# Roots of the last norms one at a time, a routing moved ahead of a sum, and a routing in four matmuls, at the end of a one-layer attention and expert kernel

## The chip, the cores and the metric

The kernel runs on one core of one Trainium2 chip. The metric is the device time of one execution in microseconds (us). Three runs of the kernel before took 838.86 us in the median, from 838.44 to 840.26. Engines are named as in the profile: PE is TensorE (matmuls), PEld its loading of weights, DVE is VectorE, ACT is ScalarE, POOL is GpSimd, SP is SyncE, which only issues DMAs here.

## What is computed

Two sequences of 512 tokens with 512 features go through one layer: attention with 32 query heads in 8 groups, a residual and a layer norm, then a feed-forward step with a small mixture of low-rank experts, a residual and a second layer norm. Everything is float32. The change lies in the last two lines of this:

```python
x = _layernorm(x + attention(x))
# feed-forward, four active experts of rank 8
y = einsum('bth,oh->bto', x, W_base) + b_base
z = einsum('bth,erh->bter', x, lora_A[active])
alpha = softmax(log(domain_prior[active] + 1e-12) + (einsum('bth,eh->bte', x, router_W) + router_b)[..., active])
x = _layernorm(x + y + einsum('bteo,bte->bto', einsum('bter,eor->bteo', z, lora_B[active]) * 2.0, alpha))
```

## The kernel before, in words

The tokens lie in eight tiles of 128 rows, four for each sequence. The attention runs as a long sequence of slots, `slot(T)`, each of which issues a little of every stage (projection, scores, exponentials, transposes through DRAM, context, output projection). The order in which instructions are issued is the order of the program text: nothing rearranges it, every engine works through its own instructions in that order and waits by semaphores for the others. Work for the feed-forward step is hung into the last slots with `put`. After the last slot a block written out by hand (from line 1020 on) finishes the last five tiles. The change is in this block and in the helpers it calls.

The tiles of the first sequence are `f0`, the last of which is `fz`. The four tiles of the second sequence finish in the order `fa[0]`, `fa[1]`, `fb`, `fc`; below they are also written fa0, fa1, fb and fc. Each tile is an `Ffn` object and goes through these steps:

- `base(c)`, for four chunks c of the features (line 686, tile `py`): x times the base weights, in two halves of 256 output columns, with the low-rank input (16 columns for each half) and the router's logits (4 columns) carried in the same matmuls. So the widths are 272 and 276.
- `logits` (L703 and L705, tiles `lg` and `nmx`): adds the prior and takes the maximum over the four experts.
- `alphas` (L712 to L717): the exponential on ACT with its sum, then on DVE the reciprocal, the scale, and two multiplications that give `zs`, the weighted low-rank activations.
- `low_rank` (L726, L727): PE transposes `zs` into a bank that all tiles share, DVE copies it to `zT`.
- `finish` (L731): two matmuls of `zT` with the second low-rank factors, added to `py`.
- `add` (L737): the sum with the residual into `y`, then `norm2.stats` (L634, L635).
- `norm2.root(lo, hi)` (L638, L639): for the columns lo to hi of a norm that several tiles share, the square root on ACT and then the reciprocal on DVE.
- `store` (L642, L764): POOL applies the norm to `y`, and SP issues the DMA of the tile to the output.

The tile `fc` is treated otherwise: `route` (L696, tile `zl`) computes only its low-rank input and logits, in eight matmuls of 16 or 20 columns, so that its `alphas` can be had early. Its product comes later in halves (`half`, `half_end`, L745 to L752, tile `ph`), with the residual added by a matmul with the identity, and its statistics are read from the bank (L755).

Square root and exponential need different function tables on ACT. A load of a table is put in front of an activation that needs another table than the one before it; it appears in the profile under the line of that activation. Copies on ACT need none.

A matmul of float32 operands appears in the profile as two records (two passes), a transpose as one.

Of the kernel before, what the change touches and what calls it, by code (L numbers as in the profile page):

```python
# [9 lines left out]
F32 = mybir.dt.float32  # L10
# [5 lines left out]
P = 128  # L16
# [13 lines left out]
def postln_layer_kernel(  # L30
# [33 lines left out]
    nc = tc.nc  # L64
    B, S, HID = x.shape
    NT = B * S // P
    TPB = S // P
    KC = HID // P
# [3 lines left out]
    EA = active.shape[0]  # L72
    EAR = EA * RK
# [44 lines left out]
    OH, ARH = O // 2, EAR // 2  # L118
    WX_COLS = OH + ARH + EA
    arT = const.tile([P, KC, EAR + EA], F32, name="arT")  # L120
# [503 lines left out]
    class Norm:  # L624
# [10 lines left out]
            nc.vector.bn_aggr(self.mv[:, i, :], st)  # L635

        def root(self, lo, hi):
            nc.scalar.activation(self.rstd[:, lo:hi], self.mv[:, lo:hi, 1], AF.Sqrt, bias=eps_sb)  # L638
            nc.vector.reciprocal(self.rstd[:, lo:hi], self.rstd[:, lo:hi])  # L639

        def apply(self, i, dst, src=None, engine=nc.vector):
# [10 lines left out]
    class Ffn:  # L652
# [28 lines left out]
        def base(self, c):  # L681
            if c == 0:
                self.new_banks()
            for n in range(2):
                w = OH + (ARH, WX_COLS - OH)[n]
                nc.tensor.matmul(  # L686
                    self.py[n][:, :w], lhsT=self.xT[:, c, :], rhs=wbT[:, c, n, :w], start=(c == 0), stop=(c == KC - 1),
                    skip_group_check=True)

        def route(self, pool, tag):  # L690

            zl = pool.tile([P, 2, WX_COLS - OH], F32, tag=tag, name="zl")
            for n in range(2):
                w = (ARH, WX_COLS - OH)[n]
                for c in range(KC):
                    nc.tensor.matmul(  # L696
                        zl[:, n, :w], lhsT=self.xT[:, c, :], rhs=wbT[:, c, n, OH : OH + w],
                        start=(c == 0), stop=(c == KC - 1))
            self.z = [zl[:, n, :] for n in range(2)]

        def logits(self):
            self.lg = self.own([P, EA], "lg")
# [272 lines left out]
    wbT = ffn_pool.tile([P, KC, 2, WX_COLS], F32, name="wbT")  # L975
# [9 lines left out]
    def tiles(ts_, banks, name):  # L985
        n = len(ts_)
        norms = Norm(ffn_pool, n, f"a{name}"), Norm(ffn_pool, n, f"f{name}")
        return [Ffn(t, bank, *norms, i) for i, (t, bank) in enumerate(zip(ts_, banks))]

    f0 = tiles(range(TPB), ((QX, QY), (QX, QY), (SC, SC), (QX, QY)), "0")  # L990
    fa = tiles([TPB + i for i in order[:2]], ((SC, SC), (WX, WY)), "1a")
# [28 lines left out]
    fz = f0[3]  # L1020
# [37 lines left out]
    fz.finish()  # L1058
    fc.transpose(*CTX)
    fz.add()  # L1060
    base(fa[1])
    fa[0].low_rank()
    fc.route(*CTX)
# [3 lines left out]
    fa[1].alphas()  # L1067
    fa[0].finish()
    fa[0].add()
    for c in range(KC):  # L1070
        fb.base(c)
        if c == 2:
            fa[1].low_rank()
    fc.low_rank()
    fa[1].finish()
    fa[1].add()
    fz.norm2.root(3, TPB)
    fa[0].norm2.root(0, 2)
    for f in (fz, *fa):
        f.store()  # L1080
    fb.logits()
    fb.alphas()
    for c in range(KC):
        fc.half(0, c)
    fc.half_end(0)
    fc.half_stats(0)
    fb.low_rank()
    for c in range(KC):
        fc.half(1, c)
# [59 lines left out]
```

## Time and profile before

| | |
|---|---|
| three runs, median (lowest to highest) | 838.86 us (838.44 to 840.26) |
| the profiled execution's own time | 839.75 us |
| its span, first to last instruction | 838.0 us |
| PE busy | 825.9 us, 99% |
| DVE busy | 595.6 us, 71% |
| ACT busy | 354.3 us, 42% |
| POOL busy | 290.1 us, 35% |
| mean granted clock of PE | 0.996 |
| table loads on ACT from 790 us to the end | 7, of 1283 ns each |

The span counts from the first to the last instruction; the execution's own time is 1.75 us longer. Times inside the profile are given in us from the start of the span. The profile has several views: the rows of the whole span; the chain of work that ended last, followed back from the last instruction through whatever released each step; a timeline of each engine, in which square brackets give the idle time of the engine before a row and what ended it; and a table by stretches, with busy time of each engine and the granted clock of PE (1.00 is full speed). Ends of matmuls are modelled, so lengths of PE's rows overlap somewhat.

### The profile page before, as it was taken

The numbers are of one execution on the slowest core, as the hardware profiler recorded it, in microseconds if no ns is written. First come the engines' busy times: TensorE is split into PE (matmuls) and PEld (weight loads), VectorE is DVE, ScalarE is ACT, GpSimd is POOL, SyncE is SP. The second block draws the span as 40 slices with busy tenths as digits, with TensorE's granted clock in tenths as the row PEclk, the third lists the DMA queues.
The fourth block names the chain that finished last, engine by engine and source line by source line (L and its number), as shares of the span: only waits on it lengthen the run. The fifth ranks groups of instructions, "written<-read, shape, count | busy, mean of one in ns | idle before, by whom it ended". The sixth has DMA issues, their size and how long they took to land.

```text
span 838.0 us, 10735 instructions
## 1 busy us (share of the span) xinstructions
PE 825.9 (99%) x3201; PEld 583.9 (70%) x3201; DVE 595.6 (71%) x1964; ACT 354.3 (42%) x1002; POOL 290.1 (35%) x318
## 2 busy tenths in 40 slices
PE   8999999999999999999999999999999999999996
PEld 5566677777777777777777777777777776655574
DVE  5468977787767967686767866687767878964535
ACT  1225454534434444444434343444435344663133
POOL 6463344233322334232332334334333523300022
PEclk9999999999999999999999999999999999999998
DMA  9126536364553556263543557274544536574211
GB/s 289 39 63 190 157 83 194 103 177 123 151 148 102 166 152 194 62 175 115 151 138 105 172 148 193 61 204 143 152 125 126 177 90 199 163 247 118 63 39 63
DMA packets 84971, 116.47 MB, mean 139 GB/s; under 512 B 6581, under 2 KB 64797, under 8 KB 82866
## 3 DMA queue, kind: packets, MB, share of 16 engines
q1 hardware_dynamic: 84258, 115.50, 48.1%
q0 software_dynamic: 448, 0.14, 0.2%
q8 instruction: 25, 0.41, 0.2%
q14 instruction: 32, 0.26, 0.1%
q10 hardware_dynamic: 208, 0.15, 0.1%
HBM read 71.73 MB, written 44.04 MB: 138 GB/s over the span
## 4 chain that ended last, share of the span: by engine, by line
PE 90%; DVE 4%; DMA 2%; ACT 1%; issue 1%; POOL 1%; SPq 0%; DVEq 0%; POOLq 0%
PE pc L544 16%; PE sc L488 13%; PE qx L429 11%; PE wx L429 11%; PE pp L355 9%; PE qy L429 8%; PE wy L429 8%; PE pv L342 6%; PE py L686 3%; PE po L615 3%; DMA pT<-db 1%; PE tp L274 1%; PE py L731 1%; DMA db<-zt 1%; DMA x_sb<-_attn_hidden_states_dram 1%
## 5 line engine op out<-in xcount | busy, mean ns | idle before, releaser
L503 ACT ACTIVATE p<-sc,nmax 128x288 f32<-128x288 f32 (+15 forms) x256 | 124.4, 486 | 253.0 <-DVE nmax L496 207.5
L496 DVE CUSTOM_DVE_ANT_0 sc<-sc,maskw 128x288 f32<-128x288 f32 (+15 forms) x256 | 114.1, 446 | 154.5 <-PE sc L488 151.7
L544 PE MATMUL pc<-pT,v 128*128 128x512 f32 x320 | 165.5, 599 | 0.6 <-DMA pT<-db 0.6
L488 PE MATMUL sc<-kT,qT 128*128 128x160 f32 (+15 forms) x512 | 162.0, 398 | 1.2 <-ACT p L503 1.1
L376 POOL TENSOR_TENSOR qT<-q,t 128x512 f32<-128x512 f32 x56 | 71.0, 1268 | 188.8 <-DVE q L375 188.8
L511 ACT ACTIVATE p<-p,den 128x288 f32<-128x288 f32 (+15 forms) x256 | 133.4, 522 | 0.1
L488 PEld LDWEIGHTS sc<-kT,qT 128*128 128x128 f32 x512 | 96.7, 190 | 30.3 <-issue 14.3
L416 POOL TENSOR_TENSOR cs<-ctxT 128x256 f32<-128x256 f32 x28 | 26.5, 948 | 196.2 <-PE wy L429 109.5
L550 ACT COPY ctxT<-pc 128x512 f32<-128x512 f32 x64 | 37.5, 586 | 124.9 <-PE pc L544 124.9
L519 DVE STREAM_TRANSPOSE zt<-p 128x128 f32<-128x128 f32 (+2 forms) x192 | 81.6, 425 | 0.0
L544 PEld LDWEIGHTS pc<-pT,v 128*128 128x128 f32 x320 | 57.0, 190 | 19.7 <-issue 5.4
L355 PE MATMUL pp<-xT,wk 128*128 128x512 f32 x128 | 65.0, 593 | 0.5 <-ACT xT L275 0.5
L342 PE MATMUL pv<-wv,xT 128*128 128x256 f32 x256 | 63.6, 379 | 0.0
L429 PE MATMUL wx<-wo,ctxT 128*128 128x256 f32 x224 | 57.7, 380 | 0.4 <-DVE den L507 0.4
L429 PE MATMUL qx<-xs,wq 128*128 128x256 f32 x224 | 58.0, 381 | 0.0
L342 PEld LDWEIGHTS pv<-wv,xT 128*128 128x128 f32 x256 | 48.5, 190 | 13.4 <-issue 6.9
L521 DVE STREAM_TRANSPOSE zt<-p 128x32 f32<-128x32 f32 (+3 forms) x256 | 57.4, 224 | 0.0
L429 PEld LDWEIGHTS qx<-xs,wq 128*128 128x128 f32 x224 | 41.4, 190 | 22.3 <-issue 16.0
L429 PEld LDWEIGHTS wx<-wo,ctxT 128*128 128x128 f32 x224 | 42.4, 190 | 13.5 <-issue 7.7
L503 ACT ACTIVATION_READ_ACCUMULATOR p<-sc,nmax 128x1 f32 x256 | 49.9, 195 | 0.0
L601 DVE TENSOR_TENSOR x_sb<-wx,x_sb 128x256 f32<-128x256 f32 x112 | 46.9, 419 | 0.0
L368 DVE SCALAR_TENSOR_TENSOR t<-q,bqkT,rope_sb 64x512 f32<-64x512 f32 x56 | 43.0, 768 | 1.3
(190 smaller groups left out, 1362.9 us busy)
## 6 DMA issues: line engine op xcount, KB each, us to landing
db<-zt SPq DMA_DIRECT2D x64, 256.0 KB, 4.1
pT<-db SPq DMA_DIRECT2D x16, 1024.0 KB, 4.8
db<-zt SPq DMA_DIRECT2D x64, 192.0 KB, 3.2
pT<-db SPq DMA_DIRECT2D x16, 768.0 KB, 4.5
wq<-in_L_attn_Wq_dram SPq DMA_DIRECT2D x20, 512.0 KB, 4.7
wo<-in_L_attn_Wo_dram SPq DMA_DIRECT2D x10, 1024.0 KB, 7.6
db<-zt SPq DMA_DIRECT2D x64, 128.0 KB, 2.4
pT<-db SPq DMA_DIRECT2D x16, 512.0 KB, 4.1
```

The source lines that it names most:

```text
L342: nc.tensor.matmul(psq["v", gg, t], lhsT=xT[:, c, ts(t, P)], rhs=wvs[gg][0][:, c, :], start=(c == 0), stop=(c == KC - 1))
L355: nc.tensor.matmul(psq[key], lhsT=wt[:, c, cols], rhs=xT[:, c, ts(b, S)], start=(c == 0), stop=(c == KC - 1))
L376: nc.gpsimd.tensor_tensor(dst, t1[:].rearrange("p (n s) -> p n s", s=BLK), t2[:].rearrange("p (n s) -> p n s", s=BLK), ALU.add)
L429: nc.tensor.matmul(ps, lhsT=wt[:, c, :], rhs=xt[:, c, :], start=start and c == 0, stop=c == CH - 1, skip_group_check=True)
L488: nc.tensor.matmul(sc[s][:, :w], lhsT=qT[u][:, i * QB + n].rearrange("p r s -> p (r s)"), rhs=kT[u][:].rearrange("p n s -> p (n s)")[:, :w ...
L496: nc.vector.tensor_tensor_reduce(sc[s][:, :w], sc[s][:, :w], maskw[:, S - w :], -SCALE, -MASKED, ALU.add, ALU.min, nmax[s])
L503: nc.scalar.activation(ptile[s][:, :w], sc[s][:, :w], AF.Exp, bias=nmax[s], scale=-1.0, accum_out=rden[s])
L511: nc.scalar.activation(ptile[s][:, :w], ptile[s][:, :w], AF.Copy, scale=rden[s])
L519: nc.vector.transpose(z[:, :, last - i : last, n, :].rearrange("p q j s -> p j q s"), ptile[s][:, : i * P])
L521: nc.vector.transpose(z[:, : n + 1, last, n, :], ptile[s][:, i * P : w])
L544: nc.tensor.matmul(psc[p], lhsT=v_sb[g // VG, b * TPB + j][:, ts(g % VG, D)], rhs=pT[p][:, :, ts(j, P)], start=(j == 0), stop=(j == i))
L601: nc.vector.tensor_tensor(into, pw[k, bank], into, ALU.add)
```

## The change

Three edits, all in what happens after the last slot:

1. The second norms of fz, fa0 and fa1 were rooted together, after all three sums: one root for fz, one for the pair fa0 and fa1. Now each has its own, put in right after (or one step after) its own sum, and each tile is stored at once. To let the ACT half and the DVE half stand in different places, `root` is split into `sqrt` and `invert`.
2. The `logits` and `alphas` of fb stood behind the sum of fa1 and the three stores. They now stand ahead of fa1's `finish` and `add`.
3. `route` of fc uses four matmuls of 36 columns, with the combined low-rank and router weights `arT`, in place of eight of 16 or 20 columns from `wbT`.

On ACT the order at the end becomes: root of fz, exponentials of fc and fa1, root of fa0, exponential of fb, root of fa1, root of fb and the rest; before, it was exponentials of fc and fa1, roots of fz and of the pair, exponential of fb, root of fb and the rest.

```diff
         def root(self, lo, hi):
+            self.sqrt(lo, hi)
+            self.invert(lo, hi)
+
+        def sqrt(self, lo, hi):
             nc.scalar.activation(self.rstd[:, lo:hi], self.mv[:, lo:hi, 1], AF.Sqrt, bias=eps_sb)
+
+        def invert(self, lo, hi):
             nc.vector.reciprocal(self.rstd[:, lo:hi], self.rstd[:, lo:hi])
...
         def route(self, pool, tag):
 
-            zl = pool.tile([P, 2, WX_COLS - OH], F32, tag=tag, name="zl")
-            for n in range(2):
-                w = (ARH, WX_COLS - OH)[n]
-                for c in range(KC):
-                    nc.tensor.matmul(
-                        zl[:, n, :w], lhsT=self.xT[:, c, :], rhs=wbT[:, c, n, OH : OH + w],
-                        start=(c == 0), stop=(c == KC - 1))
-            self.z = [zl[:, n, :] for n in range(2)]
+            zl = pool.tile([P, EAR + EA], F32, tag=tag, name="zl")
+            for c in range(KC):
+                nc.tensor.matmul(zl, lhsT=self.xT[:, c, :], rhs=arT[:, c, :], start=(c == 0), stop=(c == KC - 1))
+            self.z = [zl[:, :ARH], zl[:, ARH:]]
...
     fz.add()
+    fz.norm2.root(3, TPB)
+    fz.store()
     base(fa[1])
     fa[0].low_rank()
     fc.route(*CTX)
...
     fa[0].add()
+    fa[0].norm2.sqrt(0, 1)
     for c in range(KC):
         fb.base(c)
         if c == 2:
             fa[1].low_rank()
     fc.low_rank()
+    fa[0].norm2.invert(0, 1)
+    fa[0].store()
+    fb.logits()
+    fb.alphas()
     fa[1].finish()
     fa[1].add()
-    fz.norm2.root(3, TPB)
-    fa[0].norm2.root(0, 2)
-    for f in (fz, *fa):
-        f.store()
-    fb.logits()
-    fb.alphas()
+    fa[1].norm2.sqrt(1, 2)
     for c in range(KC):
         fc.half(0, c)
     fc.half_end(0)
     fc.half_stats(0)
+    fa[1].norm2.invert(1, 2)
+    fa[1].store()
     fb.low_rank()
```

## The prediction

> **What bounds the kernel now.** I read the whole-span rows first, then the chain that ended last over its final 30 us, then the timeline of the same stretch engine by engine, and last the table by stretches with the granted clock. PE is busy for 99% of the span, so until the last tiles nothing but a matmul decides. The change touches only the text from the last norms on (about 811 us to the end at 838.0), so its worth is read there. Tile names as in the kernel: fz is the last tile of the first sequence; fa0, fa1, fb, fc (objects fa[0], fa[1], fb, fc) are the four of the second, in the order in which they finish.
>
> The chain, in order of time: start, length, what.
>
> ```profile
> 814.77 1.70 PE zl L696 x16
> 816.47 1.06 PE py L731 x4
> 817.53 4.65 PE py L686 x12
> 822.18 0.11 PE tz L726
> 822.29 0.93 PE py L686 x4
> ...
> 824.88 0.71 DVE st L634
> ...
> 825.82 0.29 ACT rstd_f1a L638
> ...
> 826.14 1.28 ACT L712
> ...
> 827.43 0.40 ACT al L712 x2
> ```
>
> Up to 823.97 the chain is PE. Then it leaves PE: fa1's sum and statistics on DVE, a root on ACT, a table load of 1.28 us, the exponential of fb, and back to PE only at 828.62. In that time PE runs out of work, and its row says for what:
>
> ```profile
> 828.62 0.29 PE L726 MATMUL tz<-ident,zs 128*32 128x128 f32 x1 [1.26 <-DVE zs L717]
> 830.44 0.85 DVE L737 TENSOR_TENSOR y<-py,x_sb 128x256 f32<-128x256 f32 x2 [1.21 <-PE py L731]
> ```
>
> fb's base product was complete at 823.2, so its routing stood ready for 3 us and only its place in the queues held it. From fb's sum at 830.44 to the end nothing changes, so I measure the change by when that sum starts.
>
> The second finding is in the table by stretches (PE, PEld, DVE, ACT, POOL busy, then the clock); I cut it at the clock's own edges.
>
> ```profile
> 814.09:817.50 3.41, 3.41 (x25) 2.81 (x23) 0.76 (x4) 0.39 (x2) 0.00 (x0) 1.00 0.00 0
> 817.50:820.91 3.41, 3.41 (x9) 2.58 (x9) 2.73 (x13) 1.97 (x4) 0.00 (x0) 0.50 0.00 0
> 820.91:824.33 3.42, 3.42 (x17) 2.28 (x15) 1.07 (x4) 0.00 (x0) 0.00 (x0) 1.00 0.00 0
> 827.74:831.15 3.41, 2.53 (x11) 1.73 (x12) 1.97 (x8) 1.36 (x2) 3.41 (x3) 1.00 0.26 100
> ```
>
> For one stretch of 3.41 us the clock was halved. fb's first twelve passes took 4.65 us there; elsewhere sixteen take 3.70 us, 0.231 each, so twelve should take 2.78: 1.87 us lost on the chain.
>
> **The change, part by part.**
>
> *Routing of fc in four matmuls.* A float32 matmul is two passes, so 16 passes become 8, each of 36 columns. A pass of 16 or 20 columns takes 1.70/16 = 0.106 us, the same for both, and a transpose of 128 columns 1.33/12 = 0.111; so 36 columns cost 0.106 to 0.111 and the weights, not the columns, are paid for. Eight fewer: 0.85 us off PE, directly on the chain. The routing weights are now read from the array they were copied from; no new wait.
>
> *fz's root and store between exponentials.* Added on ACT: a load of the root's table and, after the root (0.29), one of the exponential's, 1.28 each. The sum of fz is done at 812.50, ACT is idle from 811.59 to 816.89 (wait of 5.30 for fc's logits). Load to 812.88, root to 813.17, load to 814.46; fc's exponential comes at 816.89 - 0.85 = 816.04. Cost nothing, with 1.6 us of cover; without that cover 2.9 us. DVE's reciprocal (0.13) falls at 813.2, ahead of a copy at 814.81: DVE waits there 2.31 us anyway. POOL's 2.08 us for fz and its store on SP's queue move from 826 to 813; both queues are empty there.
>
> *fa0's root alone.* ACT loads the root's table already at 818.74, 0.85 earlier now; the root must wait for fa0's statistics, which end at 821.08 - 0.85 = 820.23. So root 820.26 to 820.55, then the load for fb's exponential to 821.85. That load is only moved; the exponential of fb is queued behind it. One more root (0.29) and one more reciprocal (0.16) exist because fa's pair is split. After fb's exponential comes another load and the root of fa1; the load that stood there before (827.84) is the same one. So the net is two loads more, both around fz's root.
>
> *fb's routing ahead of fa1's sum.* DVE now does, after fa0's statistics (820.23): copy of fa1's zT to 820.53; copy of fc's zT; reciprocal; logits of fb; their maximum; then waits for ACT. Behind this wait on DVE stand fa1's sum and statistics, fc's first half statistics and fb's zT. Here is the sum with a full clock, every length from the rows of before:
> PE: routing of fc ends 815.6, finish of fa0 to 816.68, twelve passes of fb to 819.46, transpose, four passes to 820.50, transpose of fc at 820.55 (behind the zT copy), finish of fa1 to 821.76, fc's half 1.71 + 0.43 + 0.43 to 824.33, fb's transpose without a wait, four passes to 825.3.
> DVE: fc's zT 820.75, maximum of fb done 821.58. ACT: exponential at 821.87, bound by the load by 0.29 us. DVE, with the distances of 827.43 onward: 822.29 reciprocal, 822.49, 822.76 zs, fa1's sum 822.93, statistics 823.82 and 824.55, fc's half 824.77 (its bank is full at about 824.6), fa1's reciprocal 825.2, fb's zT 825.4 to 825.68.
> PE: finish of fb at 825.72, some 0.4 us after it could have begun: the old wait of 1.26 goes and this one comes. fb's sum follows 0.67 us later (829.77 to 830.44 before), at 826.39 instead of 830.44: 4.05 us.
> The parts: routing 0.85; half clock 1.87; the wait of 1.26 and the issue gaps around it, with the new wait of 0.4 taken off, some 1.3.
>
> *The stores.* fz, fa0 and fa1 leave POOL earlier, at about 815.4, 823.3 and 827.5; the last outputs then share the DMA engines with less. They landed in 1.7 and 1.9 us, the others in 2.0 (median), so I take 0; a gain of at most 0.2 us, no loss.
>
> **The half clock, weighed.** In the stretch before the slow one PE was "busy" throughout, but with the routing: at 0.231 us for 272 columns, 16 passes of 16 or 20 columns are 0.24 us of column work in 1.70. With finish (0.87 of columns in 1.06) and what is left of fa1's base product (0.57) and a transpose, columns filled about 1.8 of 3.41 us, half. The stretch at 827.74, with 0.88 us wholly empty, kept a clock of 1.00 and had about 0.6. [...]
>
> **The table loads, weighed.** [...] The rows show 1.28 and no drain: load at 826.14, next activation at 827.43. [...]
>
> **Numbers.** The profiled execution took 839.75 us, 838.0 of span and 1.75 around it. 839.75 - 4.05 = 835.7. That run stood 0.89 over the median of 838.86. The same reckoning without the half clock puts before at 839.75 - 1.8 = 837.95, 0.5 below the fastest run shown (838.44), so runs without the dip may be a little slower than the sum; I add half of that: **836.0**. If the median run of before had no dip, the gain is only 828.65 - 826.39 = 2.25, which gives 836.6 from 838.86: the same case within its scatter.
>
> **Rivals.**
> - *The dip stays or moves* (20%): 839.75 - 2.65 = 837.1, to 837.4 if it falls on fa1's finish as well. [...] Against: fewer thin passes are left.
> [...]
> - *Slower* (5%): one mechanism, at the four switches between fc's routing and fb's exponential. With x us for a switch fb's exponential starts at 814.06 + 4x once nothing covers them (x over 2.07). At x = 2.97 the gain is gone, from x = 3.16 the time is over 840.5, at 3.3 it is 841.1. Everything behind DVE's wait moves with it. Against: all seven loads of the tail took 1283 ns.
> - *As worked out* (64%): 835.2 to 836.9.
>
> A measurement of this kernel can tell about 0.2% from no change, 1.68 us: faster is under 837.18, slower over 840.54. Faster: all of the first case and over half of the dip's, 0.77; same 0.18; slower 0.05. The range goes from 834.9 (the scatter of before's runs below the sum) to 837.9, which leaves out the replaced wait and slower.
>
> **What would show it.** Right: no half clock between 814 and 824; the routing 8 passes in 0.85 us; fb's transpose without a wait and a wait of some 0.4 for fb's zT at its finish; fb's exponential straight behind its table load, near 821.9; 5.3 us idle of ACT filled at 811.6. Wrong: the clock at 0.50 somewhere else in the tail; a gap between a load and the next activation; fb's transpose still waiting for zs; fa1's sum on the chain behind ACT for more than 0.5 us.

## The result, and the profile after

The changed kernel took 835.70 us in the median of 9 runs (834.55 to 836.55). Before, run beside it, took 838.64 us in the median of 9 (836.8 to 841.59). The ratio is 0.9962, with a 95% interval of 0.9948 to 0.9976, so the change is clear of no change: some 3 us of 838.6. The spread shrank as well, from 4.8 us to 2.0. The profiled execution of after took 835.7 us with a span of 833.9.

The chain that ended last, of the kernel after, over the stretch that was shown of before (start, length, what):

```profile
814.58 0.82 PE zl L700 x8
815.40 1.06 PE py L733 x4
816.46 2.97 PE py L692 x12
819.42 0.11 PE tz L728
819.53 0.93 PE py L692 x4
820.46 0.11 PE tz L728
820.57 1.06 PE py L733 x4
821.63 1.92 PE ph L747 x8
...
824.61 0.22 PE tz L728
824.82 0.87 PE ph L747 x4
825.69 0.64 PE py L733 x2
826.33 0.02 issue
826.35 0.42 DVE y L739
```

The routing (zl) has 8 passes and 0.82 us where it had 16 and 1.70. fb's twelve passes take 2.97 us, not 4.65. The excursion through DVE and ACT between 823.97 and 828.62 is gone: the chain stays on PE up to fb's sum. That sum starts at 826.35 instead of 830.44.

The timeline of after shows who now waits for whom around fb's exponential:

```profile
820.35 1.28 ACT L714 ACT_TABLE_LOAD   x1
821.65 0.30 ACT L714 ACTIVATE al<-lg,nmx 128x4 f32<-128x4 f32 x1
822.53 0.26 DVE L719 TENSOR_TENSOR zs<-py,al 128x16 f32<-128x16 f32 x2
...
824.54 0.28 PE L728 MATMUL tz<-ident,zs 128*32 128x128 f32 x1
...
825.05 0.26 DVE L729 COPY zT<-tz 32x128 f32<-32x128 f32 x1
```

The exponential follows its table load by 0.02 us, so that load still sets when it runs. But zs is there at 822.79, and fb's transpose on PE comes at 824.54 with no wait in its row: PE is late now, not ACT. The zT copy is done at 825.31, before PE's chain needs it at 825.69.

The table by stretches of after. In before the clock was halved from 817.50 to 820.91, for 3.41 us, and again from 834.57 to the end; the two starts lie 17.07 us apart, five times 3.41. In after it is halved from 830.60 on, and the table is cut in steps of 3.41 us back from there; a step counted in this way is called a clock window below (one before the routing, the one with it, and two behind it):

```profile
810.11:813.53 3.42, 3.42 (x18) 2.92 (x18) 2.22 (x9) 2.67 (x4) 0.23 (x1) 1.00 0.01 2
813.53:816.94 3.41, 3.41 (x20) 2.65 (x19) 1.22 (x8) 1.17 (x3) 1.84 (x1) 1.00 0.20 76
816.94:820.35 3.41, 3.41 (x17) 2.58 (x15) 2.60 (x12) 1.97 (x4) 0.00 (x0) 1.00 0.00 1
820.35:823.77 3.42, 3.42 (x16) 2.49 (x14) 2.16 (x11) 2.96 (x4) 2.07 (x1) 1.00 0.00 0
```

The clock is full (1.00) in all of them.

### The profile page after: what moved, and what is told of

The parts are those of the page before. It is cut to its first block, busy times and chain, and to the rows that moved or that the text cites. A ratio compares the mean times of both kernels' runs of the same rounds, so it can differ in the third digit from the quotient of the medians.

```text
span 833.9 us, 10722 instructions
## 1 busy us (share of the span) xinstructions
PE 823.1 (99%) x3193; PEld 581.6 (70%) x3193; DVE 595.3 (71%) x1965; ACT 356.8 (43%) x1005; POOL 290.0 (35%) x318
## 4 chain that ended last, share of the span: by engine, by line
PE 93%; DVE 3%; ACT 1%; DMA 1%; POOL 1%; issue 1%; SPq 0%; DVEq 0%; POOLq 0%
PE pc L544 16%; PE sc L488 13%; PE qx L429 11%; PE wx L429 11%; PE pp L355 10%; PE qy L429 9%; PE wy L429 8%; PE pv L342 7%; PE py L692 3%; PE po L615 3%; PE tp L274 1%; PE py L733 1%; DMA x_sb<-_attn_hidden_states_dram 1%; DVE wt L568 0%; DMA db<-zt 0%
```

## The experiments

The runs come with one more number, the mean granted clock of each execution. One half clock of 3.41 us takes 0.5 x 3.41 / 838 = 0.002 off it. What is left under 1.000 is the half clock after the last matmul, which varies (3.30 us in the trace of after, 1.33 us in that of after once more). So an execution with 0.997 or less has most likely had a half clock in the middle of its work; this sorting is rough, since the last digit is 0.001. Before was run again beside the experiments: 839.15 us in the median of 57 runs on a first chip and 839.13 of 29 on a second. The routing alone, the routing widened, the routing undone and the roots together ran on the first, the other experiments on the second, and the three single runs at the end on a third. The ratios given below are not ratios of the medians.

**One part alone: the routing in four matmuls** (before, with only this):

```diff
-            zl = pool.tile([P, 2, WX_COLS - OH], F32, tag=tag, name="zl")
...
+            zl = pool.tile([P, EAR + EA], F32, tag=tag, name="zl")
+            for c in range(KC):
+                nc.tensor.matmul(zl, lhsT=self.xT[:, c, :], rhs=arT[:, c, :], start=(c == 0), stop=(c == KC - 1))
```

> The kernel before with one edit: the routing of fc in four matmuls of 36 columns; roots and fb's routing where they were. Theory A (thin columns cost twice: 0.85 us of weight loads on PE, and in those executions whose clock window catches them a half clock of 1.87 us): the routing takes 0.85 us less, no half clock between 810 us and fb's sum, fb's transpose still waits 1.3 us for zs; median about 837.0, with a spread like that of the kernel after (2 us), where before had 5. Theory B (the half clock has nothing to do with the routing): 0.85 us less and nothing else, 837.8, spread as before, the clock still at 0.50 in some executions.

Measured: 837.17 us (836.05 to 841.56, 14 runs), ratio to before 0.9991 (0.9978 to 1.0005). The expectation of theory A was met in the median, and not in the rest: five of the 14 had a mean clock of 0.994 to 0.997 and took 838.15 to 841.56, and the interval of the ratio includes no change. The other nine had a median of 836.81, against 837.71 for the 24 of before with more than 0.997. That is 0.90 us for eight passes fewer, with their weight loads (in the routing of before PEld is busy for 1.60 of the 1.63 us from 814.77 to 816.40). But low clocks were not gone, and two of the five, at 0.994, have room for two half clocks. PE's wait was still there in the trace of this kernel, whose own clock stayed full up to the last matmul:

```profile
824.92 0.29 PE L722 MATMUL tz<-ident,zs 128*32 128x128 f32 x1 [1.27 <-DVE zs L713]
```

So theory A was widened: an empty stretch of PE and a stretch of thin matmuls may each bring the half clock. That is inferred from the counts; no trace of this kernel shows it.

**Only the columns: the routing widened** (before, with the same eight matmuls over more columns, whose extra results are unused):

```diff
-                        zl[:, n, :w], lhsT=self.xT[:, c, :], rhs=wbT[:, c, n, OH : OH + w],
+                        zl[:, n, : lead + w], lhsT=self.xT[:, c, :], rhs=wbT[:, c, n, OH - lead : OH + w],
```

with `lead` = 108.

> The kernel before with one edit: the routing of fc keeps its eight matmuls (16 passes), but each takes some 110 columns of the base weights in front of its own, 124 and 128 columns in place of 16 and 20; the extra results are not used. PE's time for it should stay near 0.107 us a pass, 1.7 us in all, so only the column work rises, from 0.24 to 1.7 us. Theory A (the clock is halved for thin column work): no half clock in the tail, clock 0.998 or more in every execution, median 0.5 to 1 us under before, about 837.8. Theory B (not the columns): half clock as often as before, median 838.6.

Measured: 838.16 us (837.68 to 840.63, 14 runs), ratio 0.9995 (0.9985 to 1.0005); four of 14 at 0.997, with a median of 839.65, the other ten 837.91. In its trace the 16 passes take about as long as the thin ones:

```profile
815.83 1.95 PE L697 MATMUL zl<-wbT,x1T 128*128 128x124 f32 x16
817.71 1.13 PE L732 MATMUL py<-bmT,zT 33*128 33x256 f32 x4
```

From start to start 1.88 us, against 1.79 for the thin ones in before (814.61 to 816.40): 0.09 more for seven times the columns. The low clocks became fewer (4 of 14, where before had 33 of 57) but did not vanish, as theory A in its first form had said they would. The interval of the ratio includes no change here too.

**Both sources taken away from before: widened and filled.** On top of the widened routing, two matmuls of 276 columns, results unused, stand where PE waited:

```diff
     fc.half_stats(0)
+    fill = ps_ctx.tile([P, WX_COLS], F32, tag="ctx", name="fill")
+    for _ in range(2):
+        nc.tensor.matmul(fill, lhsT=fc.xT[:, 0, :], rhs=wbT[:, 0, 1, :], start=True, stop=True)
     fb.low_rank()
```

> The kernel before with the routing's eight matmuls widened to 124 and 128 columns as before in this study, and two matmuls of 276 columns more (4 passes, 0.93 us, results unused) ahead of fb's transpose, where PE waited 1.26 us. No work is taken off the path. Theory A with two sources: PE never has a thin stretch, no execution with a mean clock under 0.998, median 837.8 to 838.0 and a spread of 2 us, so lower than before although more is computed. Theory B: as many slow clocks as with the wide routing alone (4 of 14), median 838.2.

Measured: 837.74 us (837.27 to 840.28, 12 runs), ratio 0.9987 (0.9976 to 0.9997). None of the 12 was under 0.998, and eleven lie within 1.2 us; one, at 840.28 with a clock of 0.999, is not explained. This kernel does more work than before on PE, leaves the chain as it was, and its median is 1.4 us lower. Against the widened routing alone, 0 of 12 where 4 of 14 were low could still be chance (about 1 in 15).

```profile
824.90 1.20 PE L1090 MATMUL fill<-wbT,x1T 128*128 128x276 f32 x4
826.24 0.28 PE L727 MATMUL tz<-ident,zs 128*32 128x128 f32 x1
```

**The routing undone in after** (eight matmuls of 16 or 20 columns, all else as in after; the lines are those of the diff of the change, reversed):

> The kernel after with one edit undone: the routing of fc back in eight matmuls of 16 or 20 columns; roots one by one and fb's routing ahead of fa1's sum stay. Theory A: 0.85 us longer than after, and the half clock of 3.41 us is back in part of the executions, costing up to 1.4 us more there, so a median of 836.9 to 837.4 with a spread of 4 us. Theory B: 836.5, no more half clocks than the kernel after has.

Measured: 836.71 us (835.62 to 838.73, 22 runs), ratio 0.9973 (0.9964 to 0.9981). Six of 22 had 0.997, with a median of 837.69; the other 16 had 836.34. That is 1.37 us under the 837.71 of before with a full clock, without any help from the routing: the worth of the wait that went. In its trace fb's transpose waits for nothing:

```profile
825.23 0.28 PE L732 MATMUL tz<-ident,zs 128*32 128x128 f32 x1
```

The median lies a little under the range of theory A, since the half clock came in a quarter of the runs, not in half.

**After once more, beside before on the second chip:**

> The kernel after, unchanged, so that it stands beside the others and beside before on this chip. Theory A, widened by the first four runs (the half clock has two sources in before, the thin routing and the empty 1.26 us ahead of fb's transpose, and after has neither): median 835.7, no execution with a mean clock under 0.998, all within 2 us. Theory B (half clocks come with any arrangement): a few executions at 0.997 or less and 838.

Measured: 835.76 us (834.6 to 837.11, 7 runs), ratio 0.9968 (0.9956 to 0.998), none under 0.998. The spread is 2.5 us, a little more than expected.

**The order undone:**

```diff
-    fb.logits()
-    fb.alphas()
     fa[1].finish()
     fa[1].add()
+    fb.logits()
+    fb.alphas()
     fa[1].norm2.sqrt(1, 2)
```

> The kernel after with one edit undone: fb's logits and alphas stand behind fa1's sum again; the single roots and the four-matmul routing stay. Theory A (what held fb's exponential in before was the table load of 1.28 us behind the pair's root; the single root of fa0 takes that load out of the way, so either edit alone ends the wait): fb's exponential follows fa1's statistics without a load, near 823.6, zs is there when PE arrives, 835.5 to 836.2, the same as after. Theory D (the order of fb's routing is what gains): fb's transpose waits about 1 us for zs again, 836.7.

Measured: 835.97 us (834.71 to 839.81, 10 runs), ratio 0.9968 (0.9953 to 0.9982), the same as after, with two runs at 0.997 or less. In its trace the exponential now waits for its logits, not for a table, and PE's transpose has no wait on it:

```profile
823.67 0.30 ACT L714 ACTIVATE al<-lg,nmx 128x4 f32<-128x4 f32 x1 [1.67 <-DVE nmx L707]
...
824.90 0.28 PE L728 MATMUL tz<-ident,zs 128*32 128x128 f32 x1
```

Theory A was right: with the single roots in place, moving fb's routing forward gives nothing more that these runs can tell.

**The roots together again** (fb's routing stays ahead, the routing in four matmuls):

```diff
     fa[1].add()
-    fa[1].norm2.sqrt(1, 2)
+    fz.norm2.root(3, TPB)
+    fa[0].norm2.root(0, 2)
+    for f in (fz, *fa):
+        f.store()
```

with the other single roots and stores taken out.

> The kernel after with one edit undone: the roots of fz and of the pair fa0, fa1 and the three stores stand together behind fa1's sum as before; fb's routing stays ahead of fa1's sum and the routing stays in four matmuls. Four table loads fewer than after. Theory A (the order of fb's routing and the routing's matmuls are all of the gain; the single roots are neutral): fb's exponential 0.4 us earlier, since no table is to be loaded, two reciprocals ahead of fb's zT some 0.5 us later: 835.5 to 836.2, the same as after. Theory C (single roots and early stores are part of the gain): the third store ends after the last output; 836.7 or more.

Measured: 836.52 us (835.74 to 838.24, 20 runs), ratio 0.9973 (0.9965 to 0.998). This is between the two theories. Its arithmetic is as early as in after: from fa1's transpose (818.49) to the end of the last activation (830.22) it takes 11.73 us, in after 11.63 (819.26 to 830.89). What is longer is the stretch behind it: 3.9 us to the end of the span, 3.0 in after. POOL and SP's queue show one cause:

```profile
825.36 4.13 POOL L648 TENSOR_SCALAR y<-y,mv_f1a,rstd_f1a 128x512 f32<-128x512 f32 x2
```

```profile
825.41 4.93 SPq L766 DMA_DIRECT2D out_dram<-y  x4
830.43 0.40 SPq L774 DMA_DIRECT2D out_dram<-y  x1
```

POOL ends its third tile at 829.49, and the four stores go out in a row, up to the last output on the same queue. In after POOL had ended at 827.31. That last output was ready at 830.08 and left at 830.43, so at most 0.35 of the 0.84 us lies in the queue. The stores of whole tiles landed in up to 2.4 us, where those of after took 2.0; that the rest is lost in such transfers is likely, not shown.

**The roots together, their reciprocals later.** The same, but the two reciprocals and the stores (fa1, fa0, then fz) stand behind fb's zT:

```diff
     fb.low_rank()
+    fz.norm2.invert(3, TPB)
+    fa[0].norm2.invert(0, 2)
+    for f in (fa[1], fa[0], fz):
+        f.store()
```

> The kernel after with its single roots undone in another way: roots of fz and of the pair fa0, fa1 together behind fa1's sum, as before, but their two reciprocals and the three stores behind fb's zT, so that they stand in nobody's way on DVE. fb's routing stays ahead of fa1's sum, the routing in four matmuls. Four table loads fewer than after. Theory A (PE is the bound from 788 us to fb's finish, ACT's loads are covered): the same as after within 0.3 us, 835.5 to 836.0. Theory E (the loads of after do cost something that its trace hides): 835.2 or less. Theory C (late stores collide with the last output): 836.5 or more.

Measured: 837.37 us (836.78 to 837.91, 11 runs), ratio 0.998 (0.9969 to 0.999), beside after on the same chip with 835.76. Theory C was right, the others wrong. fz's tile is now the last on POOL:

```profile
828.74 2.07 POOL L648 TENSOR_SCALAR y<-y,mv_f,rstd_f 128x512 f32<-128x512 f32 x1
830.14 0.38 ACTq L774 DMA_DIRECT2D out_dram<-y  x1
831.79 0.40 SPq L774 DMA_DIRECT2D out_dram<-y  x1
```

The half of fc that ACT's queue sends goes out at 830.14. The other half, ready at 829.97, stands on SP's queue behind the store of fz, which POOL finishes at 830.81, and behind that of fb: it goes at 831.79, 1.8 us late, and the span ends 4.9 us after the last activation. With four table loads fewer and no wait on PE this kernel loses 1.6 us against after in the medians; in the traces all of the loss (4.9 us for 3.0) stands behind the arithmetic.

**Looking for the half clock behind the wait.** The first kernel of this section (routing in four, wait kept) was run and profiled three times more, to see which clock window is halved.

> The kernel before with the routing of fc in four matmuls, once more, for its trace. Fifteen executions of it have been seen, five of them with a mean clock of 0.997 or less. Theory A with two sources: if this execution has a half clock between 790 us and the end of the matmuls, it is the clock window right behind the one that holds PE's wait of 1.26 us for fb's zs, and not one behind the routing. Theory F (it comes anywhere): it lies elsewhere.

> The same kernel as the run before it, for the same question: whether a half clock, if this execution has one, follows the window with PE's wait for fb's zs (theory A with two sources) or lies elsewhere (theory F).

> The same kernel as the two runs before it, for the same question: whether a half clock, if this execution has one, follows the window with PE's wait for fb's zs (theory A with two sources) or lies elsewhere (theory F).

Measured: 836.6, 837.84 and 836.28 us, with clocks of 0.999. None had a half clock before the last matmul, so the question was not answered; that the half clocks of that kernel lie behind its wait was not seen in a trace. It rests on the counts:

| kernel | thin routing | PE waits 1.26 us | executions at 0.997 or less |
|---|---|---|---|
| before, both chips | yes | yes | 51 of 86 |
| routing in four (with the three above) | no | yes | 5 of 17 |
| routing widened | no | yes | 4 of 14 |
| after, routing undone | yes | no | 6 of 22 |
| roots together | no | no | 1 of 20 |
| after, order undone | no | no | 2 of 10 |
| widened and filled | no | no | 0 of 12 |
| after, both times | no | no | 0 of 16 |

The kernel with late roots (3 of 11) is left out, since its longer idle end lowers the mean (in its trace the clock is 0.80 from 831 to 833 us and 0.50 from there to 835): its three are 837.54 to 837.77, like its other runs.

The counts have a rival that the table leaves out. In the attention near 70 us, in text that no version changes, PE waits for a transfer (DMA) in some executions and not in others:

```profile
71.25 1.13 PE L544 MATMUL pc<-pT,v 128*128 128x512 f32 x2 [0.62 <-DMA pT<-db]
71.98 1.13 PE L544 MATMUL pc<-pT,v 128*128 128x512 f32 x2 [1.39 <-DMA pT<-db]
```

These are before and the routing widened; the second of the three single runs has 1.03 us there, which is most of what it took more than the other two, the order undone 0.93, after none. So part of the scatter has nothing to do with the change. A wait of that length could also bring half clocks of its own, perhaps in the two low runs of the order undone; no trace shows one there. It may be why the five low runs of the routing alone lie 2.76 us over the other nine, where one half clock costs at most 1.71, half of its 3.41.

## Why the prediction was right, point by point

- **The time.** Forecast 836.0, measured 835.7. In the profiled executions fb's sum came 4.09 us earlier, 0.19 of which was already there at fc's transpose (810.31 before, 810.12 after), ahead of the change; so 3.9 against the 4.05 of the sum. The medians moved by 2.9 us; the profiled execution of before stood 1.1 us over its median.
- **Routing, 0.85 us.** Right: the row fell by 0.88 us, the runs with a full clock by 0.90.
- **The wait and what stands around it, 1.3 us.** Right in size: 1.37 us by the runs with the routing undone. The new wait of 0.4 for fb's zT did not come. DVE came some 0.35 us sooner than in the sum. PE came 0.39 later (825.69 for 825.3): fc's first half took 2.98 us where the sum had 2.57, and twelve passes of fb 2.97 for 2.78. The two errors met, so that the total fits this closely is in part luck.
- **The half clock, 1.87 us.** Its end in after was forecast and came. It was worth 1.68 us in the traces (4.65 to 2.97 for the twelve passes), since these passes take longer than the 0.231 us each of the sum. The cause was half of it. That the routing's thin columns brought it, and that it would go with them, was the author's estimate from one trace, in which columns filled about half of the window ahead of it (0.49). The counts correct it: taking the routing's thinness away alone left 9 of 31 executions with a low clock, taking the wait away alone left 6 of 22, and with both gone 3 of 58 are left. The prediction had looked at one trace, and had counted the wait of 1.26 us only as lost time. Before's executions with a low clock lie 1.77 us over its others (839.48 against 837.71 on the first chip), about what one half clock costs, and pull its median up by 1.4; that this much of the gain is the half clock's is an estimate. The 2.65 us of the rival in which the dip stays, given 20%, is shown by no run: in both traces of after the clock is full up to the last matmul, and none of its 16 executions is under 0.998.
- **The gain without a half clock, 2.25 us.** By runs with a full clock, 838.18 to 835.76 on the second chip: 2.4.
- **Table loads.** Right: fb's activation follows its load by 0.02 us (821.63 to 821.65), and fz's two loads (811.42 and 813.02) hid in ACT's idle stretch, of which 1.52 us are left ahead of fc's exponential. A wait in place of the old one, given 11% for a time of 838.5 and no change, needed a dearer switch or a held-up sum of fa1. No run shows what it adds: all five loads in the tail of after took 1.28, where the slower rival would have needed 2.97 for a switch, and fa1's sum starts at 822.71, right behind zs.
- **Two edits for one wait.** The sum gave the end of the wait to fb's new place. The wait had two causes: fb's exponential was late because of its place on DVE and because of the table load behind the pair's root. With the routing in four, the single roots alone end it (order undone, 835.97), and so does the new place alone (roots together: no wait on PE). This the prediction did not see.
- **The stores, taken as 0.** Against before that was right. But the term hid a limit: had the stores stayed together, POOL's three tiles and SP's queue would have become late as soon as the rest was 4 us sooner. With roots together and late, 1.6 us of the gain is lost there, on one chip. For the roots together in their old place, the loss of 0.75 us (836.52 against 835.76) is between two chips with overlapping intervals, and rests on the trace. So, with fb's routing ahead, "one by one" pays on POOL and SP, not on ACT.

No version beat the kernel after. In its trace PE waits for nothing from fc's routing to fb's finish; what remains is the chain through DVE and ACT to the last output.

## What to carry to other kernels

Before you credit a reorder, ask how many things hold the late instruction; if two do, either cure looks like the whole one. When an end moves forward by some microseconds, check what was finishing just ahead of it on engines and queues off the path: they get no sooner by themselves (here POOL's third tile ended at 829.49 with the roots together, at 827.31 in after). And a mean over runs hides what a few of them show: sort the runs by their granted clock, and look for waits outside the changed stretch that come and go, before giving a cause to a difference of a microsecond or two.

## What the runs showed of the hardware that was not expected

A window in which PE did nothing at all is not needed for the half clock. In before it came for 3.41 us (817.50 to 820.91) behind a window in which PE's rows leave no gap (3.41 us busy of 3.41, 814.09 to 817.50), but in which columns at the full rate (0.231 us for 272) fill only 0.49. Where the matmuls end it comes too. In after, PE is busy for half of its last window and the next is halved; in after once more the last window is fuller, and the clock stays up for one window in which PE does nothing:

```profile
827.18:830.60 3.42, 1.69 (x7) 0.87 (x6) 2.50 (x10) 1.56 (x4) 0.13 (x1) 1.00 0.21 80
830.60:833.90 3.30, 0.00 (x0) 0.00 (x0) 0.15 (x1) 0.30 (x1) 0.00 (x0) 0.50 0.43 155
```

```profile
824.67:828.08 3.41, 3.12 (x12) 1.89 (x12) 2.30 (x7) 0.54 (x2) 1.57 (x1) 1.00 0.20 77
828.08:831.50 3.42, 0.00 (x0) 0.00 (x0) 1.17 (x5) 1.32 (x3) 0.00 (x0) 1.00 0.42 153
831.50:832.83 1.33, 0.00 (x0) 0.00 (x0) 0.00 (x0) 0.00 (x0) 0.00 (x0) 0.50 0.00 0
```

All 13 traces end in one of these ways: the next window is halved where columns fill 0.43 of the last one or less (eight traces), and not where they fill 0.61 or more (five). In between, windows with the wait of 1.26 us and 0.50 to 0.53 of column work kept the clock in four traces, and two windows with the wait near 70 us kept it with 0.47 and 0.49, where 0.49 in before did not. So a limit near one half is an estimate from these records, and no sharp one. It would explain why only some executions are hit, if the windows lie at random against the work, which was not shown (the edges seen are 817.50 in before, 830.60 and 831.50 in the two traces of after): by the same count, windows of 3.41 us laid at random over the tail fall under one half in about a fifth of the cases where one source is left (low clocks were 9 of 31 and 6 of 22), and in none where both are gone. Filling such a stretch with matmuls whose results nobody needs (four passes at 824.90, 1.20 us in their row) left the chain as it was, and none of 12 executions had a low clock.
